# A second engine fetches rows one by one: a graph layer whose gathers run on GpSimd

## The chip, the cores and the metric

The kernel runs on one core of one Trainium2 chip. A core has five engines with an instruction queue each: TensorE (PE; its weight loads are listed as PEld), VectorE (DVE), ScalarE (ACT), GpSimd (POOL) and SyncE (SP). They work side by side and wait for one another through semaphores. The metric is the device time of one execution in microseconds. Over ten executions the kernel before took 22305.29 us in the median (22274.21 to 22339.2).

## The reference

One layer of a graph network: 50,000 nodes with 160 numbers each, and 1,650,000 edges, sorted by their target, of which 50,000 lead from a node to itself.

```python
ss, vv = (s[src], v[src])              # a row of x for each edge: 64 scalars, 32 vectors
e0 = sh[:, 0:1]; e1 = sh[:, 1:4]       # four numbers of the edge
dot = jnp.einsum('eui,ei->eu', vv, e1)
out0 = C0 * (ss * e0 @ W1 + dot * INV3 @ W2)
p3 = (ss @ W3)[:, :, None] * e1[:, None, :] * INV3
p4 = jnp.einsum('eui,uw->ewi', vv * e0[:, :, None], W4) * INV3
p5 = jnp.einsum('eui,uw->ewi', jnp.cross(vv, e1[:, None, :]), W5) * INV6
out1 = C1 * (p3 + p4 + p5)
m_agg = jax.ops.segment_sum(concat(out0, out1), dst, num_segments=n)
h = concat(m_agg[:, :64] @ Ws, m_agg[:, 64:] mixed by Wv)
return x + jax.nn.relu(h)              # and a layer norm over the 160 numbers of a node
```

The message is linear in the row of x and in the edge's four numbers. So the kernel first sums (row times edge number) over the edges of a node, and applies the weights, multiplied together, once for each node.

## The kernel before

**Units, pairs, chunks.** Edges are taken 128 at a time, a *unit*; six units are a *group*, two groups a *pair* (12 units), four groups a *chunk*, twenty groups (ten pairs) a *super-chunk*. There are 1044 pairs and 522 chunks. A group's targets span at most 32 nodes. Nodes are finished in 391 *blocks* of 128.

**A pair.** GpSimd fetches the rows of x (`gather`, L319): one indirect DMA for each unit, 128 rows of 640 bytes, into a tile `xg` that holds the pair; the pool has four such tiles. VectorE makes the matrix `ha` of each unit (`spread`, L328 and L331): 128 edges by 4 x 32 columns, the edge's four numbers in the column of its target. TensorE multiplies (`group_sums`, L343): 12 matmuls into a PSUM tile `ps`, of which there are two, the first waiting until all the units have landed. VectorE copies `ps` transposed into `sums` (L349).

**A chunk and a block.** `apply_weights` (L579) multiplies `sums` by the weights, and the product is copied out of PSUM to `hp` (L581). For each block, `ahead` loads its 128 rows of x (`xt`, L592) and the numbers of its self-loops (`sa`, L596); `own` transposes xt on TensorE (`ptx`, L615), copies it out of PSUM to `xT` (L617), multiplies by the weights (`yx`, L623) and adds the four products up on VectorE (`t`, L627, L629); `block` adds the chunks' `hp` (`phb`, L639, L640) and begins the norm (L184 to L188). ScalarE takes the root (`rstd`, L193), VectorE scales (L197, L199), and SyncE stores the block (L735). The two PSUM copies, hp and xT, go through `evict`, which is VectorE's copy if ScalarE is in the dictionary `HELP`, and else ScalarE's.

**Sixteen packs.** The self-loops are first taken out of the edges. A *pack* (L408 to L573) is a list of small steps that read 128 pieces of 790 edges, close the gaps on VectorE (`COPY_PREDICATED`, L511), and write edges and self-loops to DRAM, row by row, through SyncE (L563; 17 store steps at the end, each with up to 16 DMAs). ScalarE takes part in it with the casts to `prow` (L427 to L429) and to `marks` (L447). The list has `None` steps too, in which nothing is done: three behind each store step. The steps of a pack are spread evenly over the pairs until it is due.

**Units that GpSimd doesn't fetch.** `HELP = {ET.SP: 72}`: SyncE fetches one unit in 72 itself, row by row. ScalarE casts the super-chunk's sources to byte offsets (`ro`, L274). `fetch`, called once for each pair, issues the batches that are planned for it; a batch of SyncE's is a load of 32 offsets (L671) and 32 DMAs of one row (L676), so that a unit takes four batches. One of ScalarE's would be 16 offsets and 16 DMAs. The plan asks for the unit of the pair q = at[-1] + 2, that is, two pairs behind the last batch. The tiles `xr` for these units come from the pool `far`, which has three.

**Order.** Work is put behind a pair by `after_pair`: for a block that is complete with pair p, `block` comes after p + 4, `do_root` p + 5, `do_store` (L197, L199) p + 6, `do_send` (L735) p + 8. SyncE issues in the order of the program (`tc.manual_schedule(engines={ET.SP})`, L799). The order on PE, VectorE, ScalarE and GpSimd is chosen by the scheduler of the framework, before the kernel runs; each engine then takes its instructions strictly in that order. In the order that it chose, the matmul that reads a row-by-row unit (`ps<-xr`) stands far behind the other 11 of its pair: six pairs later for 138 of the 173 units, four for 35. For that time one of the two `ps` tiles is held.

Of the kernel before, what the change touches and what calls it, by code (L numbers as in the profile page):

```python
# [38 lines left out]
F32 = mybir.dt.float32  # L39
# [6 lines left out]
ET = mybir.EngineType  # L46
# [3 lines left out]
P = 128  # L50
MUL0, MUL1 = 64, 32
D = MUL0 + 3 * MUL1
NK = 4
# [13 lines left out]
PG = 2  # L67
SG = 20

HELP = {ET.SP: 72}  # L70
HEAD = 100
RP = 128
RS = 16
KM = 31
# [29 lines left out]
def tile_gnn_resnorm(ctx: ExitStack, tc: tile.TileContext, x, src, dst, attr, W1, W2, W3, W4, W5, Ws, Wv, out, n_edges):  # L104
    nc = tc.nc
    N = x.shape[0]
    NBLK, NB, GA, G, NU, NG, L, NH, NR, FAR = plan(N, n_edges)
# [83 lines left out]
    def norm2(pool, mv, n):  # L191
        rstd = pool.tile([P, 1], F32, name="rstd")
        nc.scalar.activation(rstd[:n], mv[:n, 1:2], AF.Sqrt, bias=eps_t[:n])  # L193
        return rstd

    def norm3(pool, y, mv, rstd, n):
        nc.vector.reciprocal(rstd[:n], rstd[:n])  # L197
        o = pool.tile([P, D], F32, name="o")
        nc.vector.tensor_scalar(o[:n], y[:n], mv[:n, 0:1], rstd[:n], op0=ALU.subtract, op1=ALU.mult)  # L199
        return o  # L200

# [14 lines left out]
    nblocks = math.ceil(N / P)  # L216
# [7 lines left out]

    with tc.tile_pool(name="once", bufs=1) as once, tc.tile_pool(name="raw", bufs=2) as rawp, \
            tc.tile_pool(name="idx", bufs=2) as idxp, tc.tile_pool(name="rows", bufs=4) as rowp, \
            tc.tile_pool(name="far", bufs=3) as farp, \
            tc.tile_pool(name="ops", bufs=3) as op, tc.tile_pool(name="sums", bufs=4) as sump, \
            tc.tile_pool(name="hp", bufs=alive + 4) as hpp, tc.tile_pool(name="node", bufs=3) as np_, \
            tc.tile_pool(name="ahead", bufs=7) as aheadp, \  # L230
            tc.tile_pool(name="psC", bufs=1, space=PSUM) as psC, tc.tile_pool(name="psK", bufs=2, space=PSUM) as psK, \
            tc.tile_pool(name="psP", bufs=1, space=PSUM) as psP, tc.tile_pool(name="psA", bufs=2, space=PSUM) as psA, \
            tc.tile_pool(name="psM", bufs=2, space=PSUM) as psM, ExitStack() as later_pools:
# [8 lines left out]
        dq = nc.sync  # L242
# [115 lines left out]
        def row_start(r):  # L358

            lo, hi = (math.floor(r * L * (1 - 1 / degree)) - 2 * FAR - 2, math.ceil(r * L * (1 - 1 / degree)) + 2 * FAR + 2)  # L360
            return (max(lo, 0), hi if r else 0), (max(math.floor((EH + r * L) / degree) - FAR - 2, 0),
                                                  math.ceil((EH + r * L) / degree) + FAR + 2)

        edges = dram.tile([1, (row_start(NR - 1)[0][1] + L) * C], F32, name="edges")
        selves = dram.tile([1, (row_start(NR - 1)[1][1] + W) * NK], F32, name="selves")
        edge_bytes = edges.bitcast(U8).rearrange("o f -> (o f)")
        self_bytes = selves.bitcast(U8).rearrange("o f -> (o f)")
        rows_stored = [0]
# [39 lines left out]
        def pack(c):  # L408

            r0 = c * RP  # L410
            n = min(RP, NR - r0)
            e0 = EH + r0 * L
            e = slice(e0, e0 + n * L)
            steps, T = [], {}
# [154 lines left out]


            for head, j in [(False, j) for j in range(RS)] + [(True, 0)]:
                steps += [partial(store, head, j), None, None, None]
            return steps + [stored]  # L573

        def apply_weights(at, ng):
# [8 lines left out]
        def rows_of(b):  # L584
            nb = min(P, N - b * P)
            return nb, slice(b * P, b * P + nb)

        def ahead(b):

            nb, row = rows_of(b)  # L590
            xt = aheadp.tile([P, D], F32, name="xt")
            dq.dma_start(xt[:nb], x[row, :])  # L592

            assert rows_stored[0] == NR or row_start(rows_stored[0])[1][0] >= row.stop
            sa = aheadp.tile([P, NK], F32, name="sa")
            dq.dma_start(sa[:nb], selves[0, row.start * NK:row.stop * NK].rearrange("(n k) -> n k", k=NK))  # L596
            return xt, sa

        def nodes(b):

# [32 lines left out]
        def block(b, xt, t, hot2):  # L633
# [3 lines left out]
            for i, c in enumerate(cs):  # L637
# [7 lines left out]
        pairs = [(s, g, min(PG, NG - g, (s + 1) * SG - g)) for s in range(NSC)  # L645
                 for g in range(s * SG, min(NG, (s + 1) * SG), PG)]
        batches, helped = {}, {}
        for h, (eng, period) in enumerate(HELP.items()):
            first = PG * G + h * period // 2
            nbatch = P // ROWS[eng]  # L650
            while True:
                at = [int(first + i * period / nbatch) // (PG * G) for i in range(nbatch)]
                q = at[-1] + 2
                if q >= len(pairs) or pairs[q][2] < PG:
                    break
                s, g, ng = pairs[q]
                u = (g - s * SG + ng) * G - 1 - len(helped.get(q, []))
                helped.setdefault(q, []).insert(0, (eng, h))
                for i, p in enumerate(at):
                    batches.setdefault(p, []).append((eng, h, q, s, u, i))  # L660
                first += period
# [46 lines left out]
        def after_pair(p, f, *args):  # L708
            later.setdefault(p, []).append((f, args))

        hps, of_nodes, resid, rstds, outs = {}, {}, {}, {}, {}
# [4 lines left out]
                of_nodes[b] += (nodes(b),)  # L716

        def do_ahead(b):
            of_nodes[b] = ahead(b)

        def do_own(b):
            of_nodes[b] = own(b, *of_nodes.pop(b))
# [5 lines left out]
            rstds[b] = norm2(np_, resid[b][1], rows_of(b)[0])  # L728

        def do_store(b):  # L730
            outs[b] = norm3(np_, *resid.pop(b), rstds.pop(b), rows_of(b)[0])

        def do_send(b):
            nb, row = rows_of(b)
            dq.dma_start(out[row, :], outs.pop(b)[:nb])  # L735

        def do_cast(s):
            raws[s] = cast(raws[s])
# [56 lines left out]
        for at, bs in zip(complete, after):  # L795
            for b in bs:
                after_pair(max(at - AHEAD, START - 1), do_ahead, b)
                after_pair(max(at - AHEAD + 4, START), do_own, b)
        later_pools.enter_context(tc.manual_schedule(engines={ET.SP}))  # L799
        for p, (s, g, ng) in enumerate(pairs):  # L800
            if p % per == 0 and s + 1 < NSC:
                end = min(NG, (s + 2) * SG) * G * P - EH
                assert end <= 0 or rows_stored[0] == NR or end <= row_start(rows_stored[0])[0][0]
                raws[s + 1] = load(s + 1)
                after_pair(p + 1, do_cast, s + 1)
                after_pair(p + 4, do_place, s + 1)
                if s + 2 == NSC:
                    after_pair(p + 5, examine_all)
                    after_pair(p + 8, read_flags)
            rows = gather(placed[s], (g - s * SG) * G, ng * G,  # L810
                          [fetched.pop((p, h)) for _, h in helped.get(p, [])])
            if p + 1 < len(pairs):
                s1, g1, ng1 = pairs[p + 1]
                has[p + 1] = spread(placed[s1], (g1 - s1 * SG) * G, ng1 * G)
            if g % QG == 0:
                sums = sump.tile([P, ND, QG, W], F32, name="sums")
            group_sums(p, rows, has.pop(p), sums, g % QG)
            fetch(p)
            if p == START - 2:
                with ExitStack() as behind, tc.tile_pool(name="begin", bufs=1) as beginp:  # L820
                    for i in first_ones:
                        behind.enter_context(tc.issue_after(i))
                    weights(beginp, psM)
            if p == START - 1:
                with ExitStack() as behind, tc.tile_pool(name="table", bufs=1) as tablep:
                    for i in first_ones:
                        behind.enter_context(tc.issue_after(i))
                    row_table(tablep)
                nc.gpsimd.iota(place_, pattern=[[1, L]], base=1, channel_multiplier=0,
                               allow_small_or_imprecise_dtypes=True)  # L830
                nc.gpsimd.iota(chunk_, pattern=[[1, NCH]], base=0, channel_multiplier=0,
                               allow_small_or_imprecise_dtypes=True)
                packp = later_pools.enter_context(tc.tile_pool(name="pack", bufs=1))
            if packs and p >= START:
                todo = math.ceil(len(packs[0]) * min(1, (p + 1 - began) / max(1, due[0] - began)))
                for step in packs[0][done:todo]:
                    if step:
                        step()
                done = todo
                if done == len(packs[0]):  # L840
                    packs.pop(0), due.pop(0)
                    done, began = 0, p + 1
            if (g + ng) % QG == 0 or g + ng == NG:
                for b in after[c]:
                    after_pair(p + 4, do_block, b)
                    after_pair(p + 5, do_root, b)
                    after_pair(p + 6, do_store, b)
                    after_pair(p + 8, do_send, b)
                after_pair(p + 2, do_weights, c, sums, g + ng - c * QG)
                c += 1  # L850
            for f, args in later.pop(p, []):
                f(*args)
# [16 lines left out]
    with tc.tile_pool(name="up", bufs=1) as up, tc.tile_pool(name="us", bufs=2) as us, tc.For_i(0, once_more, 1):  # L869
# [16 lines left out]
        far = up.tile([PB, 2, CB, nseg], F32, name="far2")  # L886
        for s in range(nseg):
# [7 lines left out]
            for c in range(CB):  # L895
# [3 lines left out]
                at = us.tile([PB, 2, SEG], F32, name="at")  # L899
# [18 lines left out]
    with tc.tile_pool(name="edges2", bufs=2) as ep, tc.tile_pool(name="ops2", bufs=2) as op, \  # L918
            tc.tile_pool(name="node2", bufs=1) as np_, tc.tile_pool(name="psA2", bufs=2, space=PSUM) as psA, \
            tc.tile_pool(name="psF2", bufs=1, space=PSUM) as psF:  # L920
        with tc.For_i(0, blocks, 1) as b:
# [5 lines left out]
            with tc.For_i(u0, u1, GA) as u:  # L927
# [11 lines left out]
                for j in range(GA):  # L939
                    nc.gpsimd.indirect_dma_start(  # L940
                        out=xg[:, j, :], out_offset=None, in_=x,
# [29 lines left out]
            xt = np_.tile([NBLK, D], F32, name="xt2")  # L971
            nc.scalar.dma_start(xt, x[row, :])
            y, mv = norm1(np_, ph, xt, NBLK)
            o = norm3(np_, y, mv, norm2(np_, mv, NBLK), NBLK)
            nc.scalar.dma_start(out[row, :], o[:NBLK])


# [31 lines left out]
```

## Time and profile before

| what | value |
|---|---|
| median of ten executions | 22305.29 us |
| profiled execution | 22342.36 us, span 22340.5 us |
| POOL busy | 11690.1 us (52%), 12363 instructions |
| PE busy | 8720.9 us (39%) |
| VectorE busy | 6240.0 us (28%), 11070 instructions |
| ScalarE busy | 548.2 us (2%), 1497 instructions |
| granted TensorE clock | 0.652 |
| row-by-row DMAs of SyncE (L676) | 22144 |
| share of the DMA engines | 17.0% indirect, 3.0% other |

The busy time of an engine is the time inside its counted instructions. SyncE has no busy time on the page, since issuing a DMA isn't counted; its instructions are seen on the timeline. "<-remote" says that an engine was released by a semaphore that the profile can't lay to one instruction of another engine at that moment.

### The profile page before, as it was taken

Reading aid. Unit: us, or ns where it says so; the run is one execution under the profiler, and the core shown is the slowest. Engines: PE = TensorE matmul, PEld = TensorE weight load, DVE = VectorE, ACT = ScalarE, POOL = GpSimd, SP = SyncE. Lnnn points to the kernel's source line nnn. Section 1 sums busy time; section 2 is a strip of 40 time slices with the busy share of each in tenths; the row PEclk is TensorE's granted clock in tenths of the full one; section 3 lists DMA queues with packets and bytes.
Section 4 is the critical chain, followed back from the end, with each engine's and each line's share of the span. In section 5 each row is a group of like instructions: output and inputs, shape, how many; then the busy total and the mean of one; then the engine's idle time right before and its main releaser. Section 6 shows DMA issues by size and latency. Waiting matters only on the chain. (4 is left out here: it accounts for less than half of the span.)

```text
span 22340.5 us, 167279 instructions
## 1 busy us (share of the span) xinstructions
PE 8720.9 (39%) x38505; PEld 7674.2 (34%) x38506; DVE 6240.0 (28%) x11070; ACT 548.2 (2%) x1497; POOL 11690.1 (52%) x12363
## 2 busy tenths in 40 slices
PE   3343433433434333343343433333343333433334
PEld 3333333333333333333333333333333333333333
DVE  4231413213232221422313223142231313213222
ACT  0000000000000000000000000000000000000000
POOL 6455554554545455454555555555555455554555
PEclk6666666666666666666666666666666666666666
DMA  2121221221212122221122221122221122211221
GB/s 63 54 56 53 55 57 54 55 54 53 56 54 57 53 54 56 55 55 54 53 54 55 55 56 53 52 54 55 55 56 52 53 55 56 56 52 51 54 55 51
DMA packets 843237, 1218.89 MB, mean 55 GB/s; under 512 B 300227, under 2 KB 623912, under 8 KB 838262
## 3 DMA queue, kind: packets, MB, share of 16 engines
q0 software_dynamic: 592752, 1012.42, 17.0%
q1 hardware_dynamic: 248058, 194.45, 3.0%
q8 instruction: 323, 5.29, 0.1%
q14 instruction: 664, 5.44, 0.1%
q10 hardware_dynamic: 1440, 1.29, 0.0%
HBM read 1135.77 MB, written 71.40 MB: 54 GB/s over the span
## 5 line engine op out<-in xcount | busy, mean ns | idle before, releaser
L319 POOL DMA_INDIRECT xg<-in_x,si x12349 | 11685.9, 946 | 10573.8 <-PE ps L343 5022.6
L343 PE MATMUL ps<-xg,ha 128*128 128x160 f32 x24698 | 4959.2, 372 | 6562.2 <-DVE sums L349 4519.2
L343 PEld LDWEIGHTS ps<-xg,ha 128*128 128x128 f32 x24698 | 4705.4, 250 | 6805.0 <-DVE sums L349 4780.3
L349 DVE STREAM_TRANSPOSE sums<-ps 128x320 f32<-128x320 f32 x1044 | 537.1, 514 | 7755.0 <-remote 6453.0
L623 PE MATMUL yx<-BWh,xT 80*128 80x320 f32 x3128 | 1514.6, 652 | 2580.4 <-ACT xT L617 2249.6
L331 DVE TENSOR_TENSOR ha<-hot,pk 128x1536 f32<-128x1536 f32 x1044 | 1801.9, 1727 | 1287.4 <-remote 1280.4
L623 PEld LDWEIGHTS yx<-BWh,xT 80*128 80x128 f32 x3128 | 841.6, 282 | 3053.6 <-ACT xT L617 2324.6
L579 PE MATMUL phc<-BWk,sums 128*128 128x160 f32 x5220 | 1195.4, 397 | 1749.8 <-DVE sums L349 1227.9
L579 PEld LDWEIGHTS phc<-BWk,sums 128*128 128x128 f32 x5220 | 1094.4, 268 | 1854.7 <-DVE sums L349 1268.5
L639 PE MATMUL phb<-hp,hot 128*128 128x160 f32 x3474 | 829.4, 404 | 660.6 <-DVE t L629 369.2
L627 DVE TENSOR_SCALAR t<-yx,sa 128x160 f32<-128x160 f32 x391 | 149.7, 383 | 3199.2 <-PE yx L623 2445.6
L639 PEld LDWEIGHTS phb<-hp,hot 128*128 128x128 f32 x3474 | 763.6, 275 | 797.7 <-issue 399.9
L629 DVE SCALAR_TENSOR_TENSOR t<-yx,sa,t 128x160 f32<-128x160 f32 x1173 | 448.4, 382 | 926.9 <-remote 539.2
L640 DVE TENSOR_TENSOR phb<-phb,t 128x160 f32<-128x160 f32 x391 | 129.7, 332 | 1729.4 <-remote 1222.5
L615 PE MATMUL ptx<-ident,xt 128*80 128x128 f32 (+1 forms) x782 | 180.2, 319 | 966.4 <-DMA xt<-in_x 785.6
L328 DVE TENSOR_TENSOR hot<-bank,rel 128x384 f32<-128x384 f32 x1044 | 555.1, 546 | 4.0
L617 ACT COPY xT<-ptx 80x256 f32<-80x256 f32 x391 | 143.5, 367 | 12558.5 <-remote 9168.5
L511 DVE COPY_PREDICATED prow<-marks,prow 128x2370 f32<-128x2370 int32 (+8 forms) x160 | 443.8, 2774 | 0.6
L615 PEld LDWEIGHTS ptx<-ident,xt 128*80 128x80 f32 (+1 forms) x782 | 101.4, 138 | 993.2 <-issue 557.5
L511 DVE COPY_PREDICATED pra<-marks,pra 128x1580 f32<-128x1580 int32 (+8 forms) x160 | 305.3, 1908 | 0.0
L343 PE MATMUL ps<-xr,ha 128*128 128x160 f32 x346 | 106.0, 399 | 483.9 <-DMA xr<-in_x 402.7
L605 DVE TENSOR_TENSOR hot<-bank,rr 128x512 f32<-128x512 f32 (+2 forms) x391 | 288.4, 738 | 0.0
(148 smaller groups left out, 2996.1 us busy)
## 6 DMA issues: line engine op xcount, KB each, us to landing
xr<-in_x SPq DMA_DIRECT2D x22144, 0.6 KB
xg<-in_x,si POOLq DMA_INDIRECT x12349
edges<-prow SPq DMA_DIRECT2D x1994, 18.5 KB
r<-edges SPq DMA_DIRECT2D x99, 360.0 KB
selves<-mine SPq DMA_DIRECT2D x1992, 0.5 KB
xt<-in_x SPq DMA_DIRECT2D x390, 80.0 KB
out<-o SPq DMA_DIRECT2D x390, 80.0 KB
pra<-in_attr SPq DMA_DIRECT2D x15, 1580.0 KB
```

The lines of the kernel that those rows point to most:

```text
L319: got.append(nc.gpsimd.indirect_dma_start(out=xg[:, j, :], out_offset=None, in_=x, in_offset=bass.IndirectOffsetOnAxis(ap=placed[0][:, u + ...
L328: nc.vector.tensor_tensor(hot[:, :n], slotsP[:, 0:W].unsqueeze(1).to_broadcast([P, n, W]), rel[:, u:u + n].unsqueeze(2).to_broadcast([P, n ...
L331: nc.vector.tensor_tensor(ha[:, :n], hot[:, :n].unsqueeze(2).to_broadcast([P, n, NK, W]), pk[:, :, u:u + n].rearrange("p k u -> p u k").un ...
L343: mm = nc.tensor.matmul(ps[:, j // G, :], ha[:, j].rearrange("p k w -> p (k w)"), xr, start=j % G == 0, stop=j % G == G - 1)
L349: nc.vector.transpose(at[:, :, i:i + ng, :].rearrange("p b g w -> p g b w"), ps[:, :ng].rearrange("p g (b f) -> p g b f", f=FB))
L511: nc.vector.copy_predicated(what[:n, a:e], mi[:, r].unsqueeze(2).to_broadcast([n, e - a, what.shape[2]]), what[:n, a + d:e + d])
L579: nc.tensor.matmul(ph[:ng * W], at[:, b, :ng].rearrange("p g w -> p (g w)"), BWk[:, b, :], start=b == 0, stop=b == ND - 1)
L605: nc.vector.tensor_tensor(hot2[:, :len(cs)], slotsP.unsqueeze(1).to_broadcast([P, len(cs), P]), rr[:, :len(cs)].unsqueeze(2).to_broadcast( ...
L615: nc.tensor.transpose(pt[:, i, :nb], xt[:nb, i * H:(i + 1) * H], ident[:nb, :nb])
L623: nc.tensor.matmul(y[:nb], xT[:, i, :nb], BWh[:, i, ks, :], start=i == 0, stop=i == 1)
L629: nc.vector.scalar_tensor_tensor(t[:nb], y[:nb, i], sa[:nb, k:k + 1], t[:nb], op0=ALU.mult, op1=ALU.add)
L639: nc.tensor.matmul(ph[:nb], hot2[:r, i, :nb], hp[:r], start=i == 0, stop=i == len(cs) - 1)
```

## The change

- `HELP = {ET.SP: 72, ET.Activation: 72}`: ScalarE fetches one unit in 72 as well, 16 rows a batch, eight batches a unit. With that `evict` becomes VectorE's copy, and hp and xT leave PSUM on VectorE.
- ScalarE issues in the order of the program, as SyncE does.
- A row-by-row unit is asked for five pairs behind its last batch instead of two, none in the last ten pairs, and none earlier than the third pair of the super-chunk before its own. `far` holds four tiles for each of the two engines' names instead of three.
- `xt` and `sa` are loaded, and `out` is stored, for two blocks by one DMA (`BP = 2`). `ahead` has five such double tiles instead of seven single ones; the output tile `o` gets a pool of its own, with three double tiles.
- `do_store` moves from p + 6 to p + 8 and `do_send` from p + 8 to p + 10.
- The three `None` behind each store step of a pack are gone, so that a pack has some 77 steps instead of some 128.

In the order of the changed program GpSimd has 12181 gathers (before 12349). The `ps<-xr` matmul stands two pairs behind its pair for 250 of 341 units, one pair behind for 57, and with it for 34.

```diff
-HELP = {ET.SP: 72}
+HELP = {ET.SP: 72, ET.Activation: 72}
 HEAD = 100
+BP = 2
...
-    def norm3(pool, y, mv, rstd, n):
+    def norm3(o, y, mv, rstd, n):
         nc.vector.reciprocal(rstd[:n], rstd[:n])
-        o = pool.tile([P, D], F32, name="o")
         nc.vector.tensor_scalar(o[:n], y[:n], mv[:n, 0:1], rstd[:n], op0=ALU.subtract, op1=ALU.mult)
         return o
...
-            tc.tile_pool(name="far", bufs=3) as farp, \
+            tc.tile_pool(name="far", bufs=4) as farp, \
...
-            tc.tile_pool(name="ahead", bufs=7) as aheadp, \
+            tc.tile_pool(name="ahead", bufs=5) as aheadp, tc.tile_pool(name="outs", bufs=3) as outp, \
...
             for head, j in [(False, j) for j in range(RS)] + [(True, 0)]:
-                steps += [partial(store, head, j), None, None, None]
+                steps.append(partial(store, head, j))
             return steps + [stored]
...
-        def ahead(b):
-            nb, row = rows_of(b)
-            xt = aheadp.tile([P, D], F32, name="xt")
-            dq.dma_start(xt[:nb], x[row, :])
-            assert rows_stored[0] == NR or row_start(rows_stored[0])[1][0] >= row.stop
-            sa = aheadp.tile([P, NK], F32, name="sa")
-            dq.dma_start(sa[:nb], selves[0, row.start * NK:row.stop * NK].rearrange("(n k) -> n k", k=NK))
-            return xt, sa
+        def together(b):
+            bs = list(range(b // BP * BP, min(nblocks, b // BP * BP + BP)))
+            return bs if all(rows_of(i)[0] == P for i in bs) else [b]
+
+        def ahead(bs):
+            nb = rows_of(bs[0])[0]
+            n0, n1 = rows_of(bs[0])[1].start, rows_of(bs[-1])[1].stop
+            xt = aheadp.tile([P, BP, D], F32, name="xt")
+            dq.dma_start(xt[:nb, :len(bs)], x[n0:n1, :].rearrange("(h n) d -> n h d", h=len(bs)))
+            assert rows_stored[0] == NR or row_start(rows_stored[0])[1][0] >= n1
+            sa = aheadp.tile([P, BP, NK], F32, name="sa")
+            dq.dma_start(sa[:nb, :len(bs)],
+                         selves[0, n0 * NK:n1 * NK].rearrange("(h n k) -> n h k", h=len(bs), k=NK))
+            return [(xt[:, h], sa[:, h]) for h in range(len(bs))]
...
-                q = at[-1] + 2
-                if q >= len(pairs) or pairs[q][2] < PG:
+                q = at[-1] + 5
+                if q >= len(pairs) - 10:
                     break
                 s, g, ng = pairs[q]
+                at = [max(a, (s - 1) * (SG // PG) + 2) for a in at]
...
         def do_ahead(b):
-            of_nodes[b] = ahead(b)
+            bs = together(b)
+            if b == bs[0]:
+                of_nodes.update(zip(bs, ahead(bs)))
...
         def do_store(b):
-            outs[b] = norm3(np_, *resid.pop(b), rstds.pop(b), rows_of(b)[0])
+            bs = together(b)
+            if b == bs[0]:
+                outs[b] = outp.tile([P, BP, D], F32, name="o")
+            norm3(outs[bs[0]][:, b - bs[0]], *resid.pop(b), rstds.pop(b), rows_of(b)[0])
...
         def do_send(b):
-            nb, row = rows_of(b)
-            dq.dma_start(out[row, :], outs.pop(b)[:nb])
+            bs = together(b)
+            if b == bs[-1]:
+                n0, n1 = rows_of(bs[0])[1].start, rows_of(b)[1].stop
+                dq.dma_start(out[n0:n1, :].rearrange("(h n) d -> n h d", h=len(bs)),
+                             outs.pop(bs[0])[:rows_of(b)[0], :len(bs)])
...
-        later_pools.enter_context(tc.manual_schedule(engines={ET.SP}))
+        later_pools.enter_context(tc.manual_schedule(engines={ET.SP, ET.Activation}))
...
-                    after_pair(p + 6, do_store, b)
-                    after_pair(p + 8, do_send, b)
+                    after_pair(p + 8, do_store, b)
+                    after_pair(p + 10, do_send, b)
```

More of the change, by code (lines that the diff above doesn't have):

```diff
@@ L973, in tile_gnn_resnorm @@
             y, mv = norm1(np_, ph, xt, NBLK)
[L974 removed]
+            o = np_.tile([P, D], F32, name="o")
+            norm3(o, y, mv, norm2(np_, mv, NBLK), NBLK)
             nc.scalar.dma_start(out[row, :], o[:NBLK])
```

## The prediction

> **What bounds the kernel now.** I read the page's busy shares first, then its costliest groups, then the waits, and last the timeline of one pair.
>
> ```profile
> PE 8720.9 (39%) x38505; PEld 7674.2 (34%) x38506; DVE 6240.0 (28%) x11070; ACT 548.2 (2%) x1497; POOL 11690.1 (52%) x12363
> ...
> q0 software_dynamic: 592752, 1012.42, 17.0%
> q1 hardware_dynamic: 248058, 194.45, 3.0%
> ...
> L319 POOL DMA_INDIRECT xg<-in_x,si x12349 | 11685.9, 946 | 10573.8 <-PE ps L343 5022.6
> L343 PE MATMUL ps<-xg,ha 128*128 128x160 f32 x24698 | 4959.2, 372 | 6562.2 <-DVE sums L349 4519.2
> ```
>
> No engine is full, and the DMA engines are 20% busy. GpSimd has the most work, and it sits idle for almost as long, most of that for TensorE; TensorE sits idle for VectorE's copy of `ps`.
>
> ```profile
> ACT xT L617 <- remote: 9168.5, 170, 112.4
> DVE sums L349 <- remote: 6453.0, 497, 36.7
> POOL xg L319 <- PE ps L343: 5022.6, 221, 69.8
> PE ps L343 <- DVE sums L349: 4519.2, 402, 28.8
> POOL xg L319 <- issue: 3624.7, 11701, 16.8
> DVE t L627 <- PE yx L623: 2445.6, 267, 45.5
> PE ptx L615 <- DMA xt<-in_x: 785.6, 44, 45.2
> DVE o L199 <- DMA out<-o: 466.1, 53, 26.4
> ```
>
> In the waits (us in all, times, the longest) the issue row is the pause of 0.30 us behind each gather. A gather so costs 0.946 + 0.30 = 1.246 us, 12349 of them 15,387 us. The other 6,953 us of the span are GpSimd's stalls.
>
> ```profile
> 9851.58 27.41 SPq L676 DMA_DIRECT2D xr<-in_x  x26
> ...
> 9857.04 0.38 PE L615 MATMUL ptx<-ident,xt 128*80 128x128 f32 x2
> ...
> 9869.29 0.95 POOL L319 DMA_INDIRECT xg<-in_x,si  x1 [0.30 <-issue]
> 9874.50 1.75 DVE L331 TENSOR_TENSOR ha<-hot,pk 128x1536 f32<-128x1536 f32 x1 [21.89 <-remote]
> 9874.59 0.37 ACT L617 COPY xT<-ptx 80x256 f32<-80x256 f32 x1 [76.57 <-remote]
> 9874.73 0.94 POOL L319 DMA_INDIRECT xg<-in_x,si  x1 [4.50 <-remote]
> ```
>
> The timeline (start, us, engine) shows why nobody is full. TensorE has done `ptx` at 9857.4, but ScalarE gets word at 9874.6, 4.3 us after GpSimd has stopped (9870.2). While GpSimd gathers back to back, signals come late. Counted over the trace, 73% of TensorE's signals come over 1.5 us late then (median 4.9 us), and 1% while GpSimd stalls. SyncE suffers in the same way: 26 row DMAs take 27.4 us here. Over the trace its rows follow one another by 0.347 us when GpSimd has stalled for over 4.3 us, by 0.413 us over all of the stalls (10,366 rows in 4.28 ms), and by 1.09 us while it runs (11,156 rows in 12.2 ms; 0.42 us in the first 4 us of a burst, 0.73 up to 8, 1.46 up to 16, 2.36 later). SyncE never rests: its waits for others add up to under 0.6 ms. So the time is GpSimd's running time plus as much stall as SyncE's rows and the round trips of TensorE and VectorE need; each is quick only in a stall.
>
> **The change part by part**, against the profiled execution of 22,342 us, which lies 37 us above the median.
>
> *Fewer gathers.* 12349 - 12181 = 168 units of 1.246 us: **-209 us**, on GpSimd's running time.
>
> *Fewer DMAs on SyncE.* Loads and stores for two blocks take 585 of the 1173 `xt`, `sa` and `out` DMAs away, and two units fewer in its share (171 for 173) another 256: 841. They would otherwise go at 0.413 us in stalls; 209 us less running time takes 209/1.09 = 192 slots away. So (841 - 192) x 0.413 = **-268 us**. Ends: 0 if other waits hold the stalls open, -917 us if all 841 went at 1.09.
>
> *Earlier fetched units.* In the order before, the `ps<-xr` matmul stood six pairs behind its own for 138 of 173 units, so that one `ps` tile was nearly always held and the copy of one pair stood between TensorE and the next. In the order of the changed kernel it stands at most two behind. Counted in both orders, places where TensorE needs VectorE's `sums` copy within four matmuls of the one that fed it fall from 726 to 446. At 4519.2/726 = 6.2 us each, 280 fewer are worth up to 1,743 us; at the least nothing, since SyncE needs the stalls too. I take a third, **-580 us**, a choice nearer to the lower end: SyncE's row at 0.413 us is the nearest to what a stall must still hold, and its lighter work alone gives back only the 268 us. Where fewer round trips shorten the stalls further, SyncE is late next. The output tile of its own (three double tiles) also ends most of the 466 us that VectorE waited for `out`; that is within the ends.
>
> *Copies on VectorE.* The nearest rows of VectorE that read PSUM at this size are L640 (332 ns) and L627 (383 ns): 522 x 0.332 + 391 x 0.383 = 323 us, at 28% busy. What hides it is VectorE's idle time; TensorE waits for VectorE in (4519 + 1228 + 369) of 22,340 us, 27%: **+88 us**. Behind a copy that waits for a late signal stand `ha` and the next `sums` copy on VectorE, and behind those TensorE. The trips for `xT` and `hp` stay as many (501 before, 460 after), so the lower end is nothing, the upper 323 us plus the late signal of 4.9 us on those 460, 2.6 ms; near the lower, for ScalarE's waits there were late by the same signals.
>
> *Rows on ScalarE.* 170 units are 21,760 DMAs and 1,360 loads of offsets. At SyncE's mean pace (22,340 us, less 692 loads of 2.1 us, over its 27,400 DMAs: 0.76) and with 2.1 us a load this is 16.5 + 2.9 = 19.4 ms: ScalarE becomes nearly as full as SyncE. In program order its casts to `marks` and `prow` (48 places in all) now stand behind a batch of 16 rows: 2.1 + 16 x 0.347 to 2.36 us, 8 to 40 us. VectorE's `hit` waits for them, and behind it the pair's `ha` and `sums`. Before, `hit` waited 77 us for `prow` in all. I take 5 us each, **+240 us**; ends 0 and 48 x 20 = 960. The root has three pairs (64 us) until VectorE uses it instead of one: nothing; without that cover 391 roots would wait 8 us or more.
>
> *Denser stores.* Without the spacers the 272 store DMAs of a pack fall into some 14.6 pairs instead of 35: 18.6 a pair, for 7.8. With 21 rows a pair SyncE has 40 DMAs, at 0.76 us some 30 us in a pair of 21.4. It falls some 9 us a pair behind, 130 us at the end of a pack. What covers this is five pairs of lead (107 us; two before) for `xr`, and some four (86 us) for `xt`, for which TensorE waited 786 us before. What is late next is `xt`: 44 us x 16 packs = 700 us at the upper end; -785 at the lower, if the lightened rest of a pack ends the wait altogether. I take **+200 us**, since a late `xt` stalls GpSimd and so speeds SyncE up.
>
> Sum: 22,342 - 209 - 268 - 580 + 88 + 240 + 200 = 21,813, less 37 for the median: **about 21,780 us**.
>
> A rule of the Trainium skill speaks against the change: "DMA: Bandwidth & Descriptors", section "Issuing engines are not separate DMA queues", says that DMAs of several engines run interleaved on the same 16 engines and that a second issuer saves only the time to issue. The trace has the DMA engines at 20% and issuing at up to 2.36 us a row, so issuing is not small here. By the rule alone the second issuer would be worth nothing, and the sum without the 209 us would be 21,990.
>
> **The rivals.**
>
> *Both queues share what is slow (slower).* If SyncE's 1.09 us while GpSimd runs is its share of a common path, ScalarE's rows take half of it: 5,578 of SyncE's 11,156 rows move into the stalls at 0.413 us, **+2,304 us**; half of that if they share only after the first 8 us of a burst. 22,930 to 24,080, say 23,400. It decides from 22,305 - 21,780 = 525 us, 1,270 rows so moved. For it: all engines suffer at the same time. Against it: SyncE's pace at the same age of a burst is the same whether TensorE has a late signal pending (0.71 us from 4 to 8 us, 1.48 from 8 to 16) or not (0.75 and 1.55 while it works).
>
> *In-order waits eat it (slower).* The casts cost 960 instead of 240 us: 22,500. Or VectorE holds TensorE up for a late signal of 4.9 us at a third of the 460 copies, 750 us: 22,530; this decides from 107 such places (525 us). Together up to 23,250. For it: VectorE's `sums` already waits 6,453 us; against it: the 77 us of `prow` before.
>
> *Only GpSimd's saving counts.* The stalls stay as they are: 22,305 - 209 = 22,096. It lies in the forecast's own range.
>
> *TensorE's round trips were the bound.* The whole 1,743 us come: 20,620, held up by SyncE's rows to some 21,000.
>
> **How the numbers follow.** The forecast and the third rival 0.44 (own range 21,300 to 22,260), round trips in full 0.07, within 0.2% of before 0.06, in-order waits 0.19, shared path 0.24. A measurement of this kernel tells some 0.2% (45 us) from no change. Faster 0.51, same 0.06, slower 0.43. The range runs from 21,200, below which only part of the fourth rival lies, to 23,600, above which lies about a third of the first: some 0.14 are left out.
>
> **What would show it.** GpSimd's gathers at 12181, still 1.25 us apart in a burst. The wait of POOL for PE `ps` and of PE for `sums` both down by over 500 us. SyncE's rows still 1.09 us apart while GpSimd runs; under the first rival they rise to 1.5 us or more, and TensorE's waits for `xr` and `xt` grow. ScalarE's batches fill most of its timeline; under the second rival `hit` waits for ScalarE by several hundred us, or VectorE for `ptx` and `phc` as ScalarE did before. The prediction is wrong if SyncE's pace depends on ScalarE's rows, or if late signals now queue up on VectorE.

## The result

The changed kernel takes 24960.51 us in the median (24919.08 to 24979.18, 8 runs), the kernel before 22304.46 us beside it: a ratio of 1.1191 (95% interval 1.118 to 1.1201). It is slower by 2,656 us, where 21,780 us were forecast. The profiled execution has a span of 24930.8 us at a granted clock of 0.625.

From the page of the changed kernel, the busy shares, the DMA queues and the costliest groups:

```profile
PE 8543.3 (34%) x38505; PEld 7456.6 (30%) x38506; DVE 6568.7 (26%) x11983; ACT 269.5 (1%) x584; POOL 11566.0 (46%) x12195
...
q0 software_dynamic: 584688, 998.65, 15.0%
q1 hardware_dynamic: 238186, 194.25, 2.7%
q10 hardware_dynamic: 44960, 15.30, 0.3%
...
L319 POOL DMA_INDIRECT xg<-in_x,si x12181 | 11561.8, 949 | 13304.7 <-PE ps L343 7560.0
L343 PE MATMUL ps<-xg,ha 128*128 128x160 f32 x24362 | 4944.7, 369 | 6335.9 <-DVE sums L349 3344.1
```

The work is what it was meant to be: 168 gathers fewer, each as long as before, and a third busy DMA queue, ScalarE's. GpSimd's idle time grew from 10,574 to 13,305 us. The waits (us in all, times, the longest) tell for whom:

```profile
ACT rstd L194 <- DMA xr<-in_x: 11824.7, 267, 118.5
...
POOL xg L319 <- PE ps L343: 7560.0, 240, 122.6
...
ACT ro L274 <- DMA r<-edges: 3705.1, 43, 212.5
...
PE ps L343 <- DVE sums L349: 3344.1, 302, 44.6
PE ptx L622 <- DMA xt<-in_x: 2996.5, 85, 127.1
...
PE ps L343 <- DMA xr<-in_x: 2468.1, 80, 120.7
...
DVE rstd L198 <- ACT rstd L194: 894.6, 49, 45.8
```

TensorE's wait for VectorE's copy fell by 1,175 us, as foreseen. Its waits for `xt` and `xr` rose from 786 and 403 us to 2,997 and 2,468, by 4,276 us together. `xt` is SyncE's. Of TensorE's idle time before the matmuls that read `xr`, 2,463 us stand before units that SyncE fetched and 226 before ScalarE's. So SyncE is late, though it has 841 DMAs fewer. SyncE's own waits, first the largest of the changed kernel:

```profile
SPq L563 <- DMA xr<-in_x: 1720.4, 404, 24.8
SPq L684 <- DMA xr<-in_x: 1011.4, 1181, 68.0
SPq L679 <- ACT ro L274: 372.4, 25, 37.5
```

and the two largest of the kernel before:

```profile
SPq L676 <- DMA xr<-in_x: 194.0, 379, 1.4
SPq L735 <- DVE o L199: 72.2, 8, 48.6
```

SyncE now waits 2.7 ms for row transfers, before its rows (L684, L676 in the kernel before) and before its stores (L563), which read another tile and write other memory. The trace names the semaphores: each transfer of SyncE and ScalarE sets one of eight, and first waits for the transfer that set the same one before it, whichever of the two engines issued that. Laid out by that earlier transfer, 2.57 ms of SyncE's waits are for a row of ScalarE's (0.84 ms before its rows, 1.72 before its stores), and 1.63 ms of them pass before ScalarE has issued that row at all.

Counted from issue to issue over the whole trace, a row costs SyncE 1.233 us while GpSimd runs (1.062 before) and 0.508 in a stall (0.482); a store 2.658 (1.069) and 0.686 (0.482). All rows of SyncE take 18.24 ms instead of 17.44, all stores 5.01 instead of 3.35: 0.80 and 1.66 ms more, nearly what they wait for ScalarE's rows. And at the same age of a burst SyncE's rows are no slower than before where ScalarE issued nothing within 3 us, and slower where it did: 0.69 against 1.14 us from 4 to 8 us, 1.32 against 1.88 from 8 to 16, 2.01 against 2.69 later (before: 0.73, 1.46, 2.36).

### The profile page after: what moved, and what is told of

Read it like the earlier page. It is cut to its first block, busy times and chain, and to the rows that moved or that the text cites. A ratio compares the mean times of both kernels' runs of the same rounds, so it can differ in the third digit from the quotient of the medians.

```text
span 24930.8 us, 210399 instructions
## 1 busy us (share of the span) xinstructions
PE 8543.3 (34%) x38505; PEld 7456.6 (30%) x38506; DVE 6568.7 (26%) x11983; ACT 269.5 (1%) x584; POOL 11566.0 (46%) x12195
## 5 line engine op out<-in xcount | busy, mean ns | idle before, releaser
L319 POOL DMA_INDIRECT xg<-in_x,si x12181 | 11561.8, 949 | 13304.7 <-PE ps L343 7560.0
L343 PEld LDWEIGHTS ps<-xg,ha 128*128 128x128 f32 x24362 | 4621.7, 247 | 6641.8 <-DVE sums L349 3447.6
L579 PE MATMUL phc<-BWk,sums 128*128 128x160 f32 x5220 | 1042.8, 358 | 296.6 <-DVE t L636 119.5
L343 PE MATMUL ps<-xr,ha 128*128 128x160 f32 x682 | 198.1, 375 | 2720.4 <-DMA xr<-in_x 2458.4
L579 PEld LDWEIGHTS phc<-BWk,sums 128*128 128x128 f32 x5220 | 979.8, 241 | 360.2 <-issue 185.1
L343 PEld LDWEIGHTS ps<-xr,ha 128*128 128x128 f32 x682 | 135.5, 233 | 2755.5 <-issue 1668.4
L646 PE MATMUL phb<-hp,hot 128*128 128x160 f32 x3474 | 774.7, 380 | 339.6 <-DVE t L636 121.9
L624 DVE COPY xT<-ptx 80x256 f32<-80x256 f32 x391 | 160.1, 409 | 2380.1 <-PE ptx L622 1730.9
L301 PE MATMUL pk<-ident,r 120*128 120x120 f32 (+1 forms) x400 | 125.3, 385 | 936.1 <-DMA r<-edges 905.8
L581 DVE COPY hp<-phc 128x160 f32<-128x160 f32 x522 | 167.1, 320 | 893.7 <-remote 550.1
```

The lines of the kernel that those rows point to most:

```text
L319: got.append(nc.gpsimd.indirect_dma_start(out=xg[:, j, :], out_offset=None, in_=x, in_offset=bass.IndirectOffsetOnAxis(ap=placed[0][:, u + ...
L343: mm = nc.tensor.matmul(ps[:, j // G, :], ha[:, j].rearrange("p k w -> p (k w)"), xr, start=j % G == 0, stop=j % G == G - 1)
L579: nc.tensor.matmul(ph[:ng * W], at[:, b, :ng].rearrange("p g w -> p (g w)"), BWk[:, b, :], start=b == 0, stop=b == ND - 1)
L581: evict(hp[:ng * W], ph[:ng * W])
L646: nc.tensor.matmul(ph[:nb], hot2[:r, i, :nb], hp[:r], start=i == 0, stop=i == len(cs) - 1)
```

## The experiments

The runs came in five groups, each on one chip with the kernel before beside it, so only ratios within a group are compared closely. The first four chips were of another kind than the one of the result: the kernel before takes 15,677 to 15,713 us there. The last was of the result's kind (22,374 us). Theory A: ScalarE's rows slow SyncE's transfers down. Theory B: the dense stores make SyncE late. Theory C: late signals queue up on VectorE behind the copies.

**Without ScalarE's rows.**

```diff
-HELP = {ET.SP: 72, ET.Activation: 72}
+HELP = {ET.SP: 72}
-        evict = nc.vector.tensor_copy if ET.Activation in HELP else nc.scalar.copy
+        evict = nc.vector.tensor_copy
```

> The changed kernel without ScalarE's rows (12350 gathers again; copies on VectorE, two-block transfers, lead of five pairs, dense stores, both engines in program order all stay). Theory A, ScalarE's rows slow SyncE's down: most of the 2,650 us goes, 21,700 to 22,200 us, SyncE's row back at about 1.06 us while GpSimd runs (1.23 with ScalarE's rows), TensorE's waits for xt and xr below 1,500 us together (5,460). Theory B, the stores packed into 15 pairs make SyncE late: 24,000 us or more, and the store still at over 2 us each while GpSimd runs. Theory C, late signals queue up on VectorE through the copies: 24,000 or more, with VectorE's waits as in the changed kernel.

Measured: 15875.94 us, ratio 1.0126 (1.0109 to 1.0143). Of some 10.6% that the changed kernel loses on this kind of chip (below), all but 1.3% is gone; the absolute numbers of the expectation belong to the other kind. The copies are still on VectorE here, so on this kind of chip theory C falls.

**ScalarE's rows added to the kernel before.**

```diff
-HELP = {ET.SP: 72}
+HELP = {ET.SP: 72, ET.Activation: 72}
```

> The kernel before with ScalarE's entry in HELP alone: its rows are added and the two PSUM copies go to VectorE; SyncE alone in program order, lead of two pairs, stores spaced, one block a transfer. Theory A: slower than before by at least 2,000 us, 24,300 to 25,500, since the rows alone do it. Theory B: within 500 us of before, 22,000 to 22,800, since the stores are spaced. Theory C: as theory A in time, but with SyncE's row pace at 1.06 us as before.

Measured: 18403.77 us, 1.1745 (1.1723 to 1.1766). One line, which brings ScalarE's rows and the copies on VectorE, is enough; the rest of the change without the dense stores (lead, double transfers, program order, later store and send) wins back 6.2 points of it, by the next run on the same chip. SyncE's waits for rows are 6.3 ms here.

**Spaced stores.**

```diff
-                steps.append(partial(store, head, j))
+                steps += [partial(store, head, j), None, None, None]
```

> The changed kernel with the three empty steps behind each store step put back. Theory A: 24,400 to 25,000 us, a gain of 500 at most, for stores that fall on fewer rows of ScalarE. Theory B: 22,300 to 23,000.

Measured: 17441.31 us, 1.1124 (1.1105 to 1.1142). Against the changed kernel's 1.1057 (next group) the spacing doesn't help: theory B falls on this kind of chip. The 0.7 points between the two lie between two chips.

**As many instructions on ScalarE, but no transfers.** ScalarE's rows are gone (their units are gathered), the copies stay on VectorE, and in `fetch`:

```diff
+                if eng == ET.Activation:
+                    for _ in range(16):
+                        nc.scalar.copy(fill[0:1, 1:2], fill[0:1, 0:1])
+                    continue
```

> As the one without ScalarE's rows, but where a batch of 16 rows stood ScalarE does 16 copies of one number, 21,800 more instructions without a transfer. If it is the number of instructions on a second engine that slows SyncE while GpSimd runs: SyncE's row at 1.2 us, 24,000 to 25,000 us. If it is the transfers (the path of the DMA queues, or SyncE's waits for ScalarE's transfers on the shared semaphores): as without ScalarE's rows, within 1% of that run.

Measured: 15960.57 us, 1.0181 (1.0164 to 1.0198), half a per cent above the run without the rows. It is the transfers, not the instructions. On this kind of chip, that is: signals were not late in it.

**Both kernels on one chip.** No edit to either.

> The kernel before, profiled on the chip of the following runs. The first four experiments ran on a chip on which the kernel before takes 15,678 us. There signals came late nowhere, and the gather cost 946 ns as before. Both theories: near 15,680 us if it is such a chip, gathers back to back for most of the span, SyncE's row at 0.32 to 0.36 us; near 22,300 us if it is such a chip as the first.

Measured: 15676.6 us. The waits of the kernel before on this chip, GpSimd's, ScalarE's and then SyncE's:

```profile
ACT xT L617 <- PE ptx L615: 10294.6, 312, 89.5
...
POOL xg L319 <- issue: 3709.9, 12171, 0.6
...
SPq L735 <- DVE o L199: 2947.5, 146, 62.2
SPq L671 <- ACT ro L274: 590.2, 32, 71.4
```

Here GpSimd hardly waits (all but the 0.30 us pauses is 220 us), and SyncE has time: it waits 3.5 ms for VectorE's output and ScalarE's offsets. Its row costs 0.40 us.

> The changed kernel on the same chip as the kernel before. Rows of ScalarE are the cause on either kind of chip: ratio 1.10 to 1.13 to the kernel before (with the stores spaced it was 1.112, without ScalarE's rows 1.013), with over 3 ms of SyncE's waits for row transfers.

Measured: 17332.47 us, 1.1057 (1.1038 to 1.1075). SyncE's waits in the changed kernel:

```profile
SPq L684 <- DMA xr<-in_x: 2697.3, 4068, 89.6
SPq L563 <- DMA xr<-in_x: 2076.3, 597, 94.4
SPq L679 <- ACT ro L274: 341.4, 28, 22.5
SPq L750 <- DVE o L199: 219.7, 14, 31.5
```

SyncE's spare time is gone and row transfers stand in its place: a row costs it 0.53 us instead of 0.40, a store 0.96 instead of 0.46. So the loss doesn't need the late signals on which the prediction was built.

**All row-by-row units on SyncE.** From here on two forms of theory A are told apart. Theory L: the eight semaphores that the transfers of SyncE and ScalarE use in turn, in one order over both engines, make one engine wait for the other. Theory P: the two queues only share a path. The edit is the one of the first run, with

```diff
+HELP = {ET.SP: 36}
```

> The changed kernel with all row-by-row units on SyncE (one in 36), none on ScalarE, and the copies on VectorE. Theory L, the two queues take turns because every transfer waits for the one eight places before it, whichever engine that is on: one queue is no worse than two, ratio 1.05 to 1.15, about that of the changed kernel or below it, and SyncE's waits for row transfers fall below 0.6 ms. Theory P, the two queues do work side by side and only share a path: one queue with all 49,000 transfers is slower than two, ratio 1.20 or more.

Measured: 20273.49 us, 1.2931 (1.291 to 1.2953). TensorE's wait, and SyncE's largest one:

```profile
PE ps L343 <- DMA xr<-in_x: 5027.8, 201, 76.4
...
SPq L563 <- DMA edges<-prow: 110.7, 218, 1.4
```

With one queue SyncE waits for nobody and its row costs 0.40 us again, but 43,800 of them take 17.4 ms, with stores, loads and the rest 20.3 ms: the span. A second queue does save time to issue, 3 ms against this run. The ratio is in theory P's range, and the plain form of theory L (two queues are no better than one) falls. The rule of the Trainium skill that the prediction weighed ("DMA: Bandwidth & Descriptors", section "Issuing engines are not separate DMA queues") says that a second issuer saves only issuing, which is usually small; in these runs issuing is the whole span of one of them.

**Offsets on VectorE.**

```diff
-                nc.scalar.mul(ro[:n], sf, 4.0 * D)
+                nc.vector.tensor_scalar(ro[:n], sf, 4.0 * D, None, op0=ALU.mult)
```

> The changed kernel with the casts to offsets (ro) on VectorE, so that ScalarE's rows no longer stand behind a wait for SyncE's load of the edges. Theory L: ScalarE is behind less often, SyncE's waits for row transfers and the time fall, by 200 us or more on this chip. Theory P: the time stays within 0.5%, since the number of transfers stays.

Measured: 17587.25 us, 1.1215 (1.1197 to 1.1234): slower, which neither form foresaw. ScalarE now waited 3.7 ms before its loads of the offsets (in the changed kernel not at all), since the cast came late from VectorE. The wait had only moved, and the time that SyncE stood before rows not yet issued by ScalarE stayed at 2.4 ms.

**ScalarE's own waits later.**

```diff
-                    after_pair(p + 5, do_root, b)
-                    after_pair(p + 8, do_store, b)
-                    after_pair(p + 10, do_send, b)
+                    after_pair(p + 8, do_root, b)
+                    after_pair(p + 9, do_store, b)
+                    after_pair(p + 11, do_send, b)
...
-                after_pair(p + 1, do_cast, s + 1)
+                after_pair(p + 3, do_cast, s + 1)
```

with the earliest batch of a super-chunk two pairs later too.

> The changed kernel with ScalarE's own waits later in its program: the root three pairs later (store and send one later), the cast to offsets two pairs later. Theory L (each transfer waits for the one eight places before it in the program, on whichever engine, so SyncE can't run ahead of a ScalarE that waits for VectorE or for the load of the edges): those waits come when the work is long done, ScalarE and so SyncE run ahead, ratio to before 1.03 to 1.08 (1.106 for the changed kernel). Theory P (the two queues only share a path): the number of transfers stays, 1.10 to 1.11.

Measured: 17168.82 us, 1.0931 (1.0913 to 1.0949). It goes theory L's way, by 1.3 points where at least 2.6 were expected. SyncE's waits for rows fall from 4.8 to 3.6 ms, and nearly all of that is time before ScalarE had issued the row: 1.4 ms instead of 2.4.

**ScalarE with rows and roots alone** (casts to VectorE, root later as above; the edit is that of the offsets, the three lines of the root, store and send, and `nc.vector.tensor_copy` for the casts to `prow` and `marks`; the cast to offsets stays at p + 1).

> As the run with later waits for the root, and ScalarE's casts (offsets, prow, marks) on VectorE, so that ScalarE has only its rows and the roots. Theory L: as low as the run with later waits or lower, 1.02 to 1.08, less what the casts cost VectorE (16 x 6 + 32 x 0.5 + 105 x 0.4 = some 160 us, 0.01). Theory P: 1.10 to 1.12.

Measured: 17534.14 us, 1.116 (1.1142 to 1.1179). A miss for theory L. But ScalarE waited 4.9 ms for its offsets, more than in the run with the offsets on VectorE, and SyncE stood 2.4 ms before rows not yet issued, as in the changed kernel: the edit didn't take away what it was aimed at.

**Half the share on each.**

```diff
+HELP = {ET.SP: 144, ET.Activation: 144}
```

> The changed kernel with one unit in 144 on each of the two engines: as many row transfers in all as the kernel before (some 22,000), on two queues. Theory L: the second queue costs even so, 1.03 to 1.07, and SyncE still waits for row transfers by over 1 ms. Theory P: with no more transfers than before it costs no more than the run without ScalarE's rows, 1.00 to 1.015.

Measured: 15869.84 us, 1.01 (1.0083 to 1.0117), about the same as without ScalarE's rows: the ratio is theory P's, the waits are theory L's. SyncE's largest waits:

```profile
SPq L750 <- DVE o L199: 1954.1, 43, 107.0
SPq L684 <- DMA xr<-in_x: 1728.6, 1674, 110.8
SPq L750 <- DVE y L185: 1500.6, 22, 116.7
SPq L563 <- DMA xr<-in_x: 1340.9, 366, 60.1
```

SyncE still waits 3.1 ms for row transfers, 2.3 ms of which pass before ScalarE has issued the row, but also 3.5 ms for VectorE: it has time to spare, and so the waits cost little or nothing. A second queue isn't dear in itself. It is dear once it takes SyncE's last spare time.

**The kernel before, one unit in 48.**

```diff
-HELP = {ET.SP: 72}
+HELP = {ET.SP: 48}
```

> The kernel before with one unit in 48 on SyncE instead of one in 72, nothing else changed. On the second chip GpSimd's 12349 gathers of 1.246 us fill 15,390 of 15,675 us and SyncE's 22,144 rows of 0.34 us half of it, so 87 gathers fewer give 108 us: ratio 0.990 to 0.998. If SyncE's lead of two pairs is too short for three batches in two pairs: 1.00 to 1.03. On a chip like the first, where SyncE never rests: slower, 1.03 to 1.10.

Measured: 16359.9 us, 1.0411 (1.0393 to 1.0428), a miss. I had counted 0.34 us a row; with its share of offset loads and gaps a row costs SyncE 0.397 us, 33,300 take 13.2 ms, and with 1.9 ms of stores and 1.2 ms of loads and the rest SyncE is full: it waits for VectorE for only 43 us where it waited 2,948. One in 72 leaves it just enough room even on the quicker kind of chip.

**Batches of 32 on ScalarE.**

```diff
-ROWS = {ET.SP: 32, ET.Activation: 16}
+ROWS = {ET.SP: 32, ET.Activation: 32}
```

> The changed kernel with ScalarE's batches of 32 rows instead of 16, so that both engines fetch in the same pairs and the transfers of the two change places on a semaphore some 840 times instead of 1,380 (each of eight). Theory L (a row waits for the other engine's transfer eight places before it): the cost falls by a quarter or more, ratio to before 1.05 to 1.08, and SyncE's row below 0.48 us. Theory P (the number of transfers on a common path): 1.10 to 1.11, row at 0.53 us, less 0.7 ms of offset loads of ScalarE that cost nothing.

Measured: 17660.52 us, 1.1244 (1.1225 to 1.1263). Fewer places where the engines alternate, and more time: the waits are fewer and longer (row gaps of over 1 us: 353 of 5.4 us on average, in the changed kernel 710 of 3.2). How often they alternate isn't what counts. SyncE stood 3.4 ms before rows that ScalarE hadn't issued (2.4 in the changed kernel), so the run doesn't speak against the order as the cause of the waits.

**All units on ScalarE.**

```diff
+HELP = {ET.Activation: 72}
```

> The changed kernel with the row-by-row units on ScalarE alone (one in 72), none on SyncE. If only both at once are dear: 1.00 to 1.03, ScalarE's row at 0.35 to 0.45 us. If ScalarE is a slow place for rows by itself, since they stand behind its roots and casts: 1.05 to 1.12, with TensorE's waits for xr above 1 ms.

Measured: 16909.52 us, 1.0762 (1.0744 to 1.078), the second case of the expectation. SyncE has no rows at all here, some 5,000 transfers, and its waits are:

```profile
SPq L750 <- DMA xr<-in_x: 5851.3, 129, 203.6
SPq L750 <- DVE y L185: 3230.5, 100, 136.8
SPq L563 <- DMA xr<-in_x: 3159.3, 1114, 31.9
```

A store of the output (L750) waits for row transfers for up to 203.6 us, 45 us on average, though it shares no data with them, and a store of a pack costs 1.22 us instead of 0.46. Of the 5,851 us before the stores of the output, 5,697 pass before ScalarE has issued the row that had the semaphore. A path that only slows transfers down can't make SyncE wait for one that isn't on it yet; the one order can. For SyncE's long waits that shows theory L.

**The copies back on ScalarE,** without its rows: the first run with `evict = nc.scalar.copy` and `tc.manual_schedule(engines={ET.SP})`.

> The changed kernel without ScalarE's rows, with the two PSUM copies back on ScalarE and ScalarE ordered by the scheduler as before: what is left is the lead of five pairs, transfers for two blocks, dense stores, later store and send. If the copies and the program order make the 1.3% of the run without ScalarE's rows: 0.99 to 1.003. If the dense stores or the later steps make it: 1.008 to 1.015.

Measured: 15833.18 us, 1.0076 (1.0059 to 1.0093). That lies between the two cases. The copies and ScalarE's program order make some 0.5 points of the 1.3, read across two chips.

**The same with one unit in 60:** `HELP = {ET.SP: 60}`.

> As the run with the copies back, but one unit in 60 on SyncE instead of one in 72: 35 gathers fewer, 44 us less (0.003), if SyncE holds it (26,600 rows of 0.40 us, 10.6 ms, with 4 ms of the rest, under 15.3 ms): 0.003 below that run. If SyncE's in-order waits are then in the way: up to 0.02 above it.

Measured: 16051.55 us, 1.0214 (1.0197 to 1.0231): 1.4 points above, as in the second case of the expectation.

**All units on ScalarE, later waits** (the two edits above together), on a chip of the result's kind.

> The run with all row-by-row units on ScalarE, with ScalarE's own waits later in its program (root three pairs later, cast two pairs later, store and send one). Theory L (one order for the transfers of both engines): ScalarE is held up less, SyncE's waits for row transfers (9.0 ms) fall by a third or more and the ratio from 1.076 to 1.03 to 1.06. Theory P (the number of transfers on a path): 1.07 to 1.08, with SyncE's waits as they were.

Measured: 23035.67 us, 1.0297 (1.028 to 1.0314). The ratio is in theory L's range, but the chip is of the other kind, so it can't be set against 1.0762; and SyncE's waits for rows are 8.7 ms, not a third lower. Between the theories it decides nothing. But it has the copies on VectorE, the dense stores and 21,760 rows on ScalarE, and on the result's kind of chip it loses 3.0% where the changed kernel loses 11.9%. Its later waits help (1.3 points on the quick kind) and SyncE has less to do, so this is no proof, but it points at the rows of two engines beside each other and not at the copies or the dense stores.

**The rest of the change, with spaced stores** (the run with the copies back, and the three empty steps), on the same chip.

> The run with the copies back (no rows on ScalarE, ratio 1.0076) with the three empty steps behind each store step put back. If the dense stores, and with them the closer VectorE steps of a pack at other times, make the 0.8%: 1.000 to 1.003. If the lead, the transfers for two blocks or the later store make it: 1.006 to 1.010.

Measured: 23009.35 us, 1.0273 (1.0256 to 1.029), above both cases, which were set by the other kind of chip. TensorE's and GpSimd's waits, and SyncE's first:

```profile
POOL xg L319 <- PE ps L343: 5822.0, 221, 76.0
...
PE ps L343 <- DVE sums L349: 2334.0, 232, 61.1
...
PE ptx L622 <- DMA xt<-in_x: 1859.5, 62, 76.5
...
PE ps L343 <- DMA xr<-in_x: 1314.4, 52, 57.0
...
SPq L679 <- ACT ro L274: 802.7, 21, 91.9
```

This is the nearest look at the prediction's gains, on the right kind of chip and without ScalarE's rows. TensorE's wait for `sums` halved (4,519 to 2,334 us), and nothing came of it: its waits for `xt` and `xr` rose by 1,985 us, and GpSimd waits for TensorE longer than before. SyncE, which never rests on this kind of chip, now also stands 0.8 ms before offsets that ScalarE hasn't cast yet (42 us before). A batch may now be asked for right behind the cast. Which part of the change makes these 2.7% was not taken apart.

None of the versions beats the kernel before.

## Why the prediction was wrong

**What bounded the kernel** was read rightly: GpSimd's running time, and stalls as long as SyncE's rows need. The sum didn't hold to it. It priced four of six terms on other engines. The miss is 3,184 us, and the last run splits it, by ratios on chips of one kind. The parts without ScalarE's rows, its copies and the dense stores (-268 and -580) came to some +610, a miss of 1,460. The rows, the copies and the dense stores together (-209, +88, +240, +200) came to some +2,050 instead of +319, a miss of 1,730.

**Fewer gathers, -209 us: right in GpSimd's running time.** 168 fewer, 949 ns each, still 0.30 us apart.

**Fewer DMAs on SyncE, -268 us: wrong in its price.** The 841 are gone, but the term held the pace of the rest fixed. At the new pace rows and stores take 2.46 ms more, nearly as much as the whole loss (2.66 ms).

**Earlier units, -580 us: the wait fell, the time didn't.** The wait for `sums` fell by 1,175 us in the changed kernel and by 2,185 without ScalarE's rows. The step that failed is the choice that a third of the 1,743 us becomes time: TensorE's waits for SyncE's `xt` and `xr` rose by 1,985 us without ScalarE's rows and took its place. The prediction named SyncE as late next and gave it no number.

**Copies on VectorE, +88 us: not contradicted.** 0.5 points, some 80 us, on the quicker chips, together with ScalarE's program order. On the result's kind of chip, where signals come late, they were not measured alone.

**Rows on ScalarE, +240 us: the term that failed.** I counted what stands behind the rows on ScalarE, `hit` above all, and nothing that SyncE loses by them. VectorE's `hit` hardly waited (under 10 us in all); SyncE stood 2.57 ms before its own transfers until rows of ScalarE's had landed. Measured with the other parts of the change in place: 1.1057 against 1.0126 on two of the quicker chips, 9.3 points or some 1,460 us. On the result's kind of chip the changed kernel stands at 1.119, and the nearest run without ScalarE's rows, which also has the copies back and spaced stores, at 1.027. The prediction had named the sign itself: that SyncE's pace depends on ScalarE's rows. ScalarE's root, called covered, made VectorE wait 895 us as well (195 before).

**Denser stores, +200 us:** on the quicker chips dense stores were no worse than spaced ones with ScalarE's rows (1.1057 against 1.1124, on two chips). On the result's kind they were not measured alone.

**The rival "both queues share what is slow"** had the direction, the place and the cost at SyncE; its dearest case, 24,080 us, is 880 us short. Its sign at SyncE, rows 1.5 us apart while GpSimd runs, came only in part (1.233), and its mechanism is not what the traces show: the long waits are for transfers that were not yet issued, not for slow ones. The evidence against it was the wrong kind: SyncE's pace didn't depend on TensorE's late signals, but TensorE issues no transfers. No row of the trace of before had two engines issuing, and a chance of 0.24 for what no row could exclude was too small. Two things stay open: whether a common path adds to the rest of SyncE's waits (0.94 ms in the changed kernel, after ScalarE has issued), and how the 9.2 points on the result's kind of chip divide between rows, copies and dense stores.

## What to carry to other kernels

Give work to an idle engine only after asking what it issues into: ScalarE was 2% busy, and its 21,760 transfers held up SyncE, the one engine that had no time left. Put the saving beside the number of things that it costs: 209 us for 21,760 rows is 10 ns a row, and even on the quicker chip each row cost the kernel 67 ns (1,460 us in all). Look up which earlier transfer each one waits for: where two engines share semaphores in one order, the one that is late holds up the other. Where an engine never waits, count every change at that engine first; a wait that shrinks elsewhere is not time until that engine gets shorter.

## What the runs showed of the hardware

The same kernel takes 15,677 to 15,713 us on four chips and 22,304 to 22,374 us in the measurement of the result and on a fifth chip. The gather costs 946 to 947 ns on both, and the granted clock is 0.739 against 0.652. What differs is how the others fare while GpSimd gathers: on the quick kind 1% of TensorE's signals come over 1.5 us late (73% on the slow kind), and SyncE's row takes 0.34 us at any age of a burst (0.42, 0.73, 1.46 and 2.36 us). Why, no run here shows. The changed kernel loses on both kinds, by 10.6% and 11.9%.
